# Padding rows copied from HBM, later slots, a first group of four blocks and eight row buffers in a fused attention and mixture-of-experts kernel

## The chip, the core and the metric

The kernel runs on one core of a Trainium2 chip. The metric is the device time of one execution in microseconds; the time before is the median of three runs. One further execution was taken by the hardware profiler. All rows and timelines come from that one, and times in them count from the start of its span.

The core's engines work side by side: PE multiplies matrices (PEld is its weight load), DVE works on vectors, ACT evaluates functions and copies, POOL here mostly starts indirect DMAs, and SP issues the plain DMAs in order on one queue. The DMAs of SP and of POOL are carried by the same 16 DMA engines.

## The reference, cut to what matters

An input of 4 images with 256 channels and 64 x 64 pixels passes two layers. The first normalises and attends over 3 x 3 neighbourhoods. The second treats each of the 16,384 pixels as a token: a gated average over a window of 64 tokens, then a mixture of experts in which each token goes to its best two of eight experts.

```python
logits = tokens @ router_w.T
probs = softmax(logits); rw, re = top_k(probs, 2); rw = rw / rw.sum(-1)
combine = zeros((N, E)).at[arange(N), re].set(rw)
out = tokens
for e in range(E):
    h = gelu(tokens @ w1[e] + b1[e])
    y = h @ w2[e] + b2[e]
    out = out + combine[:, e:e+1] * y
```

All of it is float32.

## The kernel before, in words

**Blocks.** The pixels are cut into 32 blocks (NB) of 512 tokens. A main loop over steps g = 0 to 33 interleaves four generators at their `yield`s: `attend(g)` (first layer), `tail(g - 1)` (window average, store of the block into `out`, choice of experts), `ranks(g - 2)` and `produce(g + 1)`.

**Dispatch.** `ranks` computes for each of a block's 1,024 token-expert pairs a row in an HBM buffer `rows_in`. The buffer has two colours (U = 2) with eight expert regions each, so that the two pairs of one token stand in places that don't collide later. POOL scatters the token rows there with eight indirect DMAs per block (L869, 128 rows each). A row, 1,088 B, holds the 256 values, eight weights and eight copies of the token's number.

**Slots.** The expert work is cut into 136 slots of 256 rows. The generator `experts()` takes slot after slot through these operations, each for a different slot in one pass m:

- `fetch(m + 4)`: SP reads the slot's place from a table and loads its rows into one of seven row buffers `sx` (L1010). It waits until that buffer's former slot has been added.
- `matrix` and `pixels` (m + 2): ACT copies the expert's weights; PE transposes the rows (L1034).
- `hidden(m + 1)`: PE and ACT, first weight and GELU (L1046, L1052).
- `add(m - 1)`: POOL adds two halves of 128 rows to `out` with indirect DMAs (L1082). Each waits until the same half of the slot before has landed.
- `output(m)`: PE second weight (L1065), DVE bias and token weight (L1069, L1070).

A pass has four `yield`s; the passes m = -2 and -1 have two.

**Groups and tables.** A slot's place is known only when enough blocks have been counted. GROUPS gives the number of blocks after which `ranks` writes a new table (L913 to L961): 3, eleven times 2, seven times 1. A group's blocks yield four slots each; the first group has eight fewer, the last 16 more, 20 in all (slots 116 to 135).

**Padding.** Behind the last token row of each of the 16 regions, rows may be fetched that no token fills. In the last block's `ranks`, SP reads 16 places (`values_load`, L898, from `pad`, written at L895) and writes 136 rows of zeros, with token numbers past the end of `out`, to each (L902). Eight copies come from the SBUF tile `blank`, eight from `zeros`, which DVE fills at L794. The fetches of the last group wait for these 16 and for the dispatches.

**Pace.** `follow(at)` runs `experts()` from the main loop. The list `knots` gives, for a position in steps, how many slots are due; between knots it is interpolated. With `done` counting yields:

```python
begins = [at + 2 + LAG for at in first_of[1:]] + [NB + 2.0]
knots = [(at, max(0, n - FETCH - 1)) for at, n in zip(begins, first_slot)]
...
while done < 2 * U * due:
    done += 1
    next(stream, None)
```

FETCH is 2 and LAG 0.35. A step has 26 positions, step 32 has 14 and step 33 eight. What is left of `experts()` is run after the loop. The order on each engine follows this order of the program.

Of the kernel before, what the change touches and what calls it, by code (L numbers as in the profile page):

```python
# [47 lines left out]
FP = mybir.dt.float32  # L48
# [5 lines left out]
P = 128  # L54
# [9 lines left out]
def hybrid_block_kernel(ctx: ExitStack, tc: tile.TileContext, ins: dict, out: bass.AP):  # L64
    nc = tc.nc
    x = ins["x"]
    B, C, HW = x.shape
    W = 64
    NC = C // P
    TB = 512  # L70
    NT = TB // P
    NBI = HW // TB
    NB = B * NBI
    E = ins["w1b"].shape[0]
# [8 lines left out]
    FETCH = 2  # L83
    I32, U32 = mybir.dt.int32, mybir.dt.uint32
    ENG = mybir.EngineType
    GROUPS = (3, *[2] * 11, *[1] * 7)
    assert sum(GROUPS) == NB
    first_of = [sum(GROUPS[:k]) for k in range(len(GROUPS))]
    where = [(k, j) for k, n in enumerate(GROUPS) for j in range(n)]

    U = 2
    UP = U * P
    slots_of = [2 * n * TB // UP for n in GROUPS]
    slots_of[0] -= E
    slots_of[-1] += 2 * E
    assert slots_of[0] > 0
    first_slot = [sum(slots_of[:k]) for k in range(len(GROUPS) + 1)]
    SLOTS = max(slots_of)
    N = B * HW

    PAD = P + E
# [3 lines left out]
    RW = C + 2 * E  # L105
# [7 lines left out]
    w1p = ctx.enter_context(tc.tile_pool(name="w1p", bufs=1))  # L113
    w2p = ctx.enter_context(tc.tile_pool(name="w2p", bufs=2))
    w3p = ctx.enter_context(tc.tile_pool(name="w3p", bufs=3))
    w4p = ctx.enter_context(tc.tile_pool(name="w4p", bufs=4))
    rowp = ctx.enter_context(tc.tile_pool(name="rowp", bufs=7))
    w1sp = ctx.enter_context(tc.tile_pool(name="w1sp", bufs=3))
    hbm = ctx.enter_context(tc.tile_pool(name="hbm", bufs=1, space=bass.MemoryType.DRAM))
    ps_a = ctx.enter_context(tc.tile_pool(name="ps_a", bufs=5, space=PSUM))  # L120
# [140 lines left out]
    for n in range(4):  # L261
        t = const.tile([P, NK + 3], FP, tag=f"logits_{n}", name=f"logits_{n}")
# [36 lines left out]
    def iota(name, shape, pattern, base=0, by_partition=0):  # L299
        t = const.tile(shape, FP, tag=name, name=name)  # L300
        nc.gpsimd.iota(
            t, pattern=pattern, base=base, channel_multiplier=by_partition,
            allow_small_or_imprecise_dtypes=True,
        )
        return t
# [9 lines left out]
    place = iota("place", [P, NT], [[P, NT]], by_partition=1)  # L315
# [15 lines left out]
    blank = const.tile([P, U, RW], FP, tag="blank", name="blank")  # L331
# [3 lines left out]
        float(N),  # L335
    )
    rows_in = hbm.tile([U * HALF, RW], FP, tag="rows_in", name="rows_in")

    def rows_at(at):

        return rows_in.rearrange("(t n) r -> n t r", t=U)[bass.ds(at, P)]
# [100 lines left out]
    def produce(g):  # L442
# [25 lines left out]
        for j in range(0 if i == 0 else 1, NT + 1):  # L468
# [13 lines left out]
        ct[g] = qdotb  # L482
        H = P // 2
        nc.scalar.activation(
            qdotb[0:H, 0:1], first[H:P, C : C + 1], AF.Identity, bias=qbk[H:P]
        )
        nc.scalar.activation(
            qdotb[0:H, 1:NT], v[H:P, 0 : NT - 1, C], AF.Identity, bias=qbk[H:P]
        )
        nc.scalar.activation(qdotb[H:P, :], v[0:H, :, C], AF.Identity, bias=qbk[0:H])  # L490

# [29 lines left out]
    sums, table, norm1 = {}, {}, {}  # L521
# [4 lines left out]
    nc.vector.memset(earlier, 0.0)  # L526
    dispatched = {k: [] for k in range(len(GROUPS))}
    latest = []
# [83 lines left out]
    def tail(g):  # L612
# [143 lines left out]
        both = w2p.tile([P, NT, PAIRS], FP, tag="both", name=f"both_{g}")  # L756
        H, D = E // 2, E // 2 - 1
        at = chosen[:, :, 0, :]
# [4 lines left out]
        )  # L763
        nc.vector.tensor_mul(both[:, :, D * E :], at[:, :, 0:H], at[:, :, H:])

# [18 lines left out]
    def ranks(g):  # L784
        if not 0 <= g < NB:
            return
        k, j = where[g]
        n_blocks = GROUPS[k]
        hot = hots.pop(g)
        chosen, tok = chosens.pop(g), tokens.pop(g)  # L790
        if g == NB - 1:

            zeros = w2p.tile([P, NC, TB], FP, tag="q", name="zeros")
            nc.vector.memset(zeros[:, :, 0:RW], 0.0)  # L794
            nc.vector.tensor_scalar_add(
                zeros[:, :, C + E : RW].bitcast(U32),
                place[:, 0:U].unsqueeze(2).to_broadcast([P, U, E]), float(N + UP),
            )

        yield  # L800

# [16 lines left out]
        nc.vector.tensor_single_scalar(colour[:, :, 1], odd.bitcast(I32), 1, op=ALU.bitwise_and)  # L818
        nc.vector.tensor_scalar(colour[:, :, 0], colour[:, :, 1], -1.0, 1.0, ALU.mult, ALU.add)

        each = w2p.tile([P, 2, NT, U, E], FP, tag="each", name=f"each_{g}")
        for c in range(2):
            nc.vector.tensor_mul(
                each[:, c], hot[:, c].unsqueeze(2).to_broadcast([P, NT, U, E]),
                colour.unsqueeze(3).to_broadcast([P, NT, U, E]),
            )
        by_colour = w2p.tile([P, NT, U * E], FP, tag="by_colour", name=f"by_colour_{g}")
        nc.vector.tensor_add(
            by_colour, *(each[:, c].rearrange("p t k e -> p t (k e)") for c in range(2))
        )  # L830
# [26 lines left out]
        def dispatch(inst):  # L857

            for i in range(k + 1):
                tc.declare_no_dep(  # L860
                    inst, group=f"dispatch_{i}", reason="no two tokens have one row"
                )
            tc.declare_no_dep(inst, group="fetch", reason="fetched rows are not written again")
            tc.add_to_no_dep_group(f"dispatch_{k}", inst)
            dispatched[k].append(inst)
            return inst
# [24 lines left out]
        if final:  # L891


            pad = w2p.tile([1, U * E], I32, tag="pad", name=f"pad_{k}")
            nc.vector.tensor_copy(pad, so_far[0:1, NT, :])  # L895
            H = PAD // U
            for e in range(U * E):
                at = nc.values_load(  # L898
                    pad[0:1, e : e + 1], engines=[ENG.SP], min_val=0, max_val=U * HALF - PAD,
                    skip_runtime_bounds_check_because=IN_RANGE,  # L900
                )
                dispatch(nc.sync.dma_start(  # L902
                    rows_in[bass.ds(at, PAD), :].rearrange("(t p) r -> p t r", p=H),
                    (blank, zeros[:, :, 0:RW])[e // E][0:H],
                ).ins)
            yield

# [41 lines left out]
        )  # L949
        which = small("which", (1, SLOTS))[:, 0:n_slots]  # L950
        nc.vector.tensor_reduce(which, past, AX.X, ALU.add)
        tab = table[k] = w3p.tile([1, 2, SLOTS], I32, tag="tab", name=f"tab_{k}")
        nc.vector.tensor_scalar_min(tab[:, 0, 0:n_slots], which, float(E - 1))
        yield
        nc.vector.tensor_mul(past, past, step.unsqueeze(1).to_broadcast(by_e))
# [170 lines left out]
        pass  # L1126


    STEPS, LAG = {NB: 14, NB + 1: 8}, 0.35
    begins = [at + 2 + LAG for at in first_of[1:]] + [NB + 2.0]  # L1130
    knots = [(at, max(0, n - FETCH - 1)) for at, n in zip(begins, first_slot)]
    stream, done = experts(), 0

# [13 lines left out]
    for g in range(NB + 2):  # L1147
        load_xs(g + AHEAD + 2)
        channel_stats(g + AHEAD)
        gens = [attend(g), ranks(g - 2), tail(g - 1), produce(g + 1)]  # L1150
        if g == 1:
            load_experts()
        n = 0
        while gens:
            for gen in list(gens):
                if next(gen, gens) is gens:
                    gens.remove(gen)
                    continue
                n += 1
                follow(g + min(n / STEPS.get(g, 26), 0.999))  # L1160
# [51 lines left out]
```

## Time and profile before

| What | us |
|---|---|
| median of three runs (1409.02 to 1416.77) | 1412.17 |
| the profiled execution | 1381.8 |
| its span, first to last instruction | 1379.3 |
| PE busy in it | 1248.3 |
| DVE busy | 1051.8 |
| ACT busy | 878.4 |
| POOL busy | 750.7 |
| start of the first slot's fetch (L1010) | 172.3 |
| start of the last add into `out` (L1082) | 1370.5 |

How to read it: a busy time is a sum over the whole span, which has stages with different limits. PE's last matmul ends at about 1355, while the adds go on past 1370. In timeline rows the columns are start, duration, engine, line, operation, out<-in, count, and in brackets the idle time before it and what ended it. Where a wait for several things is put down to an engine, it is the one that came last by the profile; if that engine had long been done, it was another, often a DMA. Rows with SPq are what SP's queue did. Rows of chains give start, duration and what. Rows of stretches give the stretch, its length, the busy time and count of each engine, PE's granted clock as a share of full speed, the busy share of the 16 DMA engines and the bytes they moved.

### The profile page before, as it was taken

How to read it: one execution, taken by the hardware profiler on the slowest of the kernel's cores; microseconds unless marked ns; L12 is line 12 of the kernel's file. 1: busy time of each engine (PE TensorE's matmuls, PEld its weight loads, DVE VectorE, ACT ScalarE, POOL GpSimd, SP SyncE). 2: the span in 40 equal slices, each digit the busy share in tenths (PEclk: the TensorE clock that was granted, in tenths of full speed). 3: DMA queues.
4: the chain of work that ended last, by engine and by line, in shares of the span. 5: the costliest groups of instructions: out<-in, count | busy, mean ns of one | idle time of the engine just before them, and what ended most of it. 6: DMA issues, size and time to landing. Idle time of an engine off the chain costs nothing. (4 is left out here: it accounts for less than half of the span.)

```text
span 1379.3 us, 24259 instructions
## 1 busy us (share of the span) xinstructions
PE 1248.3 (91%) x6380; PEld 999.0 (72%) x6380; DVE 1051.8 (76%) x5159; ACT 878.4 (64%) x1699; POOL 750.7 (54%) x619
## 2 busy tenths in 40 slices
PE   5988797999999999999999999999999999844982
PEld 4766576787787877878888777777877777634762
DVE  4488989898888887888979897888778889721331
ACT  1454466777777778777777776777866776522430
POOL 2004324465655665665666665656666566753665
PEclk8999999999999999999999999999999999976996
DMA  9723345456665666566665645565664555655664
GB/s 320 259 72 118 126 145 158 117 137 149 154 158 131 163 149 149 142 168 138 149 163 115 143 115 139 118 149 135 149 145 83 121 106 131 127 135 108 111 107 49
DMA packets 148679, 191.43 MB, mean 139 GB/s; under 512 B 13760, under 2 KB 122816, under 8 KB 148416
## 3 DMA queue, kind: packets, MB, share of 16 engines
q0 software_dynamic: 51456, 71.34, 29.1%
q1 hardware_dynamic: 94592, 117.10, 27.9%
q10 hardware_dynamic: 2496, 1.45, 0.4%
q8 instruction: 53, 0.87, 0.3%
q14 instruction: 82, 0.67, 0.2%
HBM read 98.59 MB, written 91.25 MB: 138 GB/s over the span
## 5 line engine op out<-in xcount | busy, mean ns | idle before, releaser
L1082 POOL DMA_INDIRECT out<-sx x272 | 451.4, 1660 | 388.6 <-DVE sx L1070 103.8
L869 POOL DMA_INDIRECT rows_in<-tok,rows x256 | 254.4, 994 | 160.0 <-issue 81.7
L1065 PE MATMUL psy<-w,h 128*128 x1088 | 287.9, 387 | 5.8 <-DVE sx L1069 5.4
L1046 PE MATMUL psh<-xc,w1s 128*128 128x256 f32 x1088 | 267.6, 384 | 0.0
L1065 PEld LDWEIGHTS psy<-w,h 128*128 128x128 f32 x1088 | 200.2, 191 | 58.6 <-DVE sx L1069 16.0
L1046 PEld LDWEIGHTS psh<-xc,w1s 128*128 128x128 f32 x1088 | 199.9, 192 | 23.2 <-issue 0.5
L1069 DVE TENSOR_TENSOR sx<-psy,b2b 128x256 f32<-128x256 f32 x272 | 113.9, 419 | 127.5 <-PE psy L1065 121.4
L1052 ACT ACTIVATE h<-psh,w1s 128x256 f32<-128x256 f32 x272 | 114.5, 470 | 100.3 <-PE psh L1046 97.0
L471 PE MATMUL psv<-vo,x 128*128 128x257 f32 x528 | 132.4, 394 | 15.0 <-DVE x L453 13.1
L1034 PE MATMUL ptx<-ident,sx 128*128 128x128 f32 x544 | 84.5, 277 | 56.1 <-DMA sx<-rows_in 55.8
L1038 ACT COPY xc<-ptx 128x512 f32<-128x512 f32 x136 | 80.0, 588 | 81.3 <-PE ptx L1034 81.1
L497 PE MATMUL psq<-x,qk 128*128 128x512 f32 x256 | 126.5, 603 | 0.0
L556 PE MATMUL pss<-x,q 128*128 128x256 f32 x512 | 124.9, 387 | 0.7 <-ACT xc L624 0.7
L1034 PEld LDWEIGHTS ptx<-ident,sx 128*128 128x128 f32 x544 | 66.1, 143 | 79.4 <-DMA sx<-rows_in 35.7
L471 PEld LDWEIGHTS psv<-vo,x 128*128 128x128 f32 x528 | 100.5, 197 | 31.2 <-DVE x L453 10.5
L593 PE MATMUL psc<-v,pT 128*128 128x256 f32 x512 | 121.5, 379 | 0.0
L593 PEld LDWEIGHTS psc<-v,pT 128*128 128x128 f32 x512 | 96.7, 189 | 27.5 <-issue 13.9
L624 ACT COPY xc<-ptx 128x512 f32<-128x512 f32 x64 | 34.3, 589 | 123.8 <-PE ptx L621 123.8
L556 PEld LDWEIGHTS pss<-x,q 128*128 128x128 f32 x512 | 92.4, 190 | 24.3 <-issue 9.7
L1070 DVE TENSOR_SCALAR sx<-sx 128x256 f32<-128x256 f32 x272 | 97.7, 359 | 2.3
L1052 ACT ACT_TABLE_LOAD x77 | 98.8, 1283 | 1.0
L597 DVE SCALAR_TENSOR_TENSOR xT<-psc,den,xT 128x256 f32<-128x256 f32 x128 | 55.8, 475 | 54.2 <-PE psc L593 53.9
(212 smaller groups left out, 2424.3 us busy)
## 6 DMA issues: line engine op xcount, KB each, us to landing
sx<-rows_in SPq DMA_DIRECT2D x136, 272.0 KB
xs<-in_x SPq DMA_DIRECT2D x32, 512.0 KB
xT<-in_xT SPq DMA_DIRECT2D x32, 512.0 KB
out<-xT SPq DMA_DIRECT2D x32, 512.0 KB
x<-in_x SPq DMA_DIRECT2D x24, 640.0 KB
x<-in_x SPq DMA_DIRECT2D x8, 576.0 KB
out<-sx POOLq DMA_INDIRECT x272, 4.2
rows_in<-tok,rows POOLq DMA_INDIRECT x256, 2.6
```

The lines of the kernel that those rows point to most:

```text
L471: nc.tensor.matmul(ps, t[:, ci, j * P : (j + 1) * P], vo[:, ci, :], start=(ci == 0), stop=(ci == NC - 1),)
L497: nc.tensor.matmul(ps, qk[:, ci, co * P : (co + 1) * P], t[:, ci, W : W + TB], start=(ci == 0), stop=(ci == NC - 1),)
L556: nc.tensor.matmul(ps, q[:, ci, t * P : (t + 1) * P], t_[:, ci, t * P : t * P + NK], start=(ci == 0), stop=(ci == NC - 1),)
L593: nc.tensor.matmul(ps[:, u, :], pT[:, u, j, :], vals[j], start=(j == 0), stop=(j == 1))
L869: return nc.gpsimd.indirect_dma_start(out=rows_in[:, :], out_offset=bass.IndirectOffsetOnAxis(ap=rows[:, c, t : t + 1], axis=0), in_=tok[: ...
L1034: nc.tensor.transpose(pt[:, c, t * P : (t + 1) * P], xs[:, t, c * P : (c + 1) * P], ident)
L1046: nc.tensor.matmul(ps[:, f, :], w1s[:, o : o + P], xc[:, ci, :], start=(ci == 0), stop=(ci == NC - 1),)
L1052: inst = nc.scalar.activation(h[:, f, :], ps[:, f, :], AF.Gelu, bias=w1s[:, F1 + f : F1 + f + 1])
L1065: nc.tensor.matmul(ps[:, t, :], h[:, f, t * P : (t + 1) * P], w2[:, e, f, :], start=(f == 0), stop=(f == NC - 1),)
L1069: nc.vector.tensor_add(ys[:, t, :], ps[:, t, :], b2b[:, e, :])
L1070: nc.vector.tensor_scalar_mul(ys[:, t, :], ys[:, t, :], xs[:, t, bass.ds(e + C, 1)])
L1082: inst = nc.gpsimd.indirect_dma_start(out=out, out_offset=bass.IndirectOffsetOnAxis(ap=xs[:, t, C + E : C + E + 1].bitcast(U32), axis=0), ...
```

## The change

Four things are changed. (1) The padding rows stand ready in HBM: at the start two fillers of 136 rows are built in SBUF (POOL and DVE) and written to a new HBM tensor; the 16 pads of the last block copy from there, both sides seen as 17 rows of 8,704 B. The tile `zeros` is gone. (2) The knots lie later and later: a group's slots begin 2.35 steps behind its last block for the first group and 3.0 for the last but one. (3) The first group has four blocks and eight slots, and six single blocks follow in place of seven, so 18 groups in place of 19; there are still 136 slots, the last 20 in the last group. (4) There are eight row buffers in place of seven. To fit, `each` and `by_colour` have one buffer in place of two; `tab` has four in place of three.

```diff
-    GROUPS = (3, *[2] * 11, *[1] * 7)
+    GROUPS = (4, *[2] * 11, *[1] * 6)
...
-    rowp = ctx.enter_context(tc.tile_pool(name="rowp", bufs=7))
+    rowp = ctx.enter_context(tc.tile_pool(name="rowp", bufs=FETCH + 6))
...
+    filler = hbm.tile([U, PAD, RW], FP, tag="filler", name="filler")
+    for k in range(U):
+        t = w2p.tile([P, NC, TB], FP, tag="q", name=f"filler_{k}")[0 : PAD // U, :, 0:RW]
+        nc.gpsimd.memset(t, 0.0)
+        nc.vector.tensor_scalar_add(
+            t[:, :, C + E :].bitcast(U32),
+            place[0 : PAD // U, 0:U].unsqueeze(2).to_broadcast([PAD // U, U, E]),
+            float(N + k * UP),
+        )
+        nc.sync.dma_start(filler[k].rearrange("(t p) r -> p t r", t=U), t)
...
-        if g == NB - 1:
-
-            zeros = w2p.tile([P, NC, TB], FP, tag="q", name="zeros")
-            nc.vector.memset(zeros[:, :, 0:RW], 0.0)
-            nc.vector.tensor_scalar_add(
-                zeros[:, :, C + E : RW].bitcast(U32),
-                place[:, 0:U].unsqueeze(2).to_broadcast([P, U, E]), float(N + UP),
-            )
...
-        each = w2p.tile([P, 2, NT, U, E], FP, tag="each", name=f"each_{g}")
+        each = w1p.tile([P, 2, NT, U, E], FP, tag="each", name=f"each_{g}")
...
-        by_colour = w2p.tile([P, NT, U * E], FP, tag="by_colour", name=f"by_colour_{g}")
+        by_colour = w1p.tile([P, NT, U * E], FP, tag="by_colour", name=f"by_colour_{g}")
...
-            H = PAD // U
             for e in range(U * E):
...
                 dispatch(nc.sync.dma_start(
-                    rows_in[bass.ds(at, PAD), :].rearrange("(t p) r -> p t r", p=H),
-                    (blank, zeros[:, :, 0:RW])[e // E][0:H],
+                    *(r.rearrange("(a b) r -> a (b r)", b=E)
+                      for r in (rows_in[bass.ds(at, PAD), :], filler[e // E]))
                 ).ins)
...
-        tab = table[k] = w3p.tile([1, 2, SLOTS], I32, tag="tab", name=f"tab_{k}")
+        tab = table[k] = w4p.tile([1, 2, SLOTS], I32, tag="tab", name=f"tab_{k}")
...
-    STEPS, LAG = {NB: 14, NB + 1: 8}, 0.35
-    begins = [at + 2 + LAG for at in first_of[1:]] + [NB + 2.0]
+    STEPS, LAST = {NB: 14, NB + 1: 8}, len(GROUPS) - 2
+    begins = [at + 2.35 + 0.65 * k / LAST for k, at in enumerate(first_of[1:])] + [NB + 2.0]
```

## The prediction

> **What bounds the kernel now.** I read the busy time of the engines by stretches first, to find the stage in which time is lost.
>
> ```profile
> core 0: us, PE busy (x) PEld busy (x) DVE busy (x) ACT busy (x) POOL busy (x), PEclk, DMA share, GB/s
> ...
> 500.00:700.00 200.00, 198.10 (x1033) 158.07 (x1033) 172.27 (x849) 150.94 (x282) 122.51 (x93) 1.00 0.62 147
> ```
>
> From about 250 to 1150 us PE is busy 99% of the time at full clock: nothing outside PE can be worth anything there. The same view of the last stage shows where PE stands still.
>
> ```profile
> 1215.00:1225.00 10.00, 8.11 (x38) 6.18 (x36) 3.88 (x10) 3.66 (x8) 7.87 (x8) 1.00 0.68 165
> 1225.00:1235.00 10.00, 0.00 (x0) 0.00 (x0) 0.00 (x0) 0.00 (x0) 4.50 (x4) 0.65 0.53 127
> ...
> 1259.00:1290.00 31.00, 30.99 (x152) 27.23 (x153) 11.26 (x28) 14.19 (x29) 15.53 (x11) 0.95 0.57 105
> 1290.00:1340.00 50.00, 41.68 (x205) 34.14 (x203) 17.05 (x41) 21.64 (x43) 30.98 (x20) 1.00 0.68 110
> ```
>
> The chain that ended last tells why:
>
> ```profile
> 1206.80 7.28 DMA out<-sx x2
> 1214.28 0.37 SPq L1010
> ...
> 1237.60 6.44 DMA rows_in<-zeros
> 1244.04 0.29 issue
> 1244.33 10.86 DMA out<-sx x3
> 1255.46 3.50 DMA sx<-rows_in
> 1259.01 1.12 PE ptx L1034 x4
> ```
>
> From 1214.7 to 1245 SP reads 16 places (L898) and issues 16 pads (L902, 144.5 KB each). The final group's first fetch waits until all have landed (1255.46), PE until 1259.01: 35.3 us of idle.
>
> But PE is not what ends last. Each slot has two adds into `out`, and each add waits for the landing of the same half of the slot before. Counting the 272 adds back from the end (slots 0 to 135; the final group is 116 to 135), POOL's timeline gives for slots 110 to 115, first halves only:
>
> ```profile
> 1226.94 1.60 POOL L1082 DMA_INDIRECT out<-sx  x1 [0.30 <-issue]
> ...
> 1236.60 1.55 POOL L1082 DMA_INDIRECT out<-sx  x1 [6.18 <-DMA out<-sx]
> ...
> 1244.33 1.55 POOL L1082 DMA_INDIRECT out<-sx  x1 [4.13 <-DMA rows_in<-zeros]
> ...
> 1251.66 1.56 POOL L1082 DMA_INDIRECT out<-sx  x1 [3.23 <-DMA out<-sx]
> ...
> 1264.92 1.55 POOL L1082 DMA_INDIRECT out<-sx  x1 [9.19 <-DVE sx L1070]
> ...
> 1269.44 1.55 POOL L1082 DMA_INDIRECT out<-sx  x1 [1.12 <-DVE sx L1070]
> ```
>
> Slot 135 begins at 1368.19, so from slot 114 on a slot takes (1368.19 - 1264.92) / 21 = 4.92 us. PE needs 3.9 (transposes at 1263.63, 1267.52, 1271.41). So adds, not PE, set the pace of the tail: 4.4 to 4.5 us a slot at the very end without fetches, up to 5.5 beside them; I use 5.0. The 38.0 us from slot 110 to 114 hold 18 more than four slots at 5.0. **That 18, not the 35 of PE, is what removing the stall can give.**
>
> **The pads.** The change lets each pad copy 17 runs of 8,704 B from HBM to HBM in place of 68 partitions of two 1,088 B rows. In the stretch 1229 to 1255 us the DMA view says:
>
> ```profile
> q0 software_dynamic: 1033, 1.02, 30.4%
> q1 hardware_dynamic: 1567, 1.66, 19.6%
> ```
>
> q1 (SP's) uses 19.6% of 16 engines for 26 us: 81.5 engine-us for 1.66 MB, 20.4 GB/s per engine. The Trainium skill, "DMA: Bandwidth & Descriptors", section "Why a DMA increments its semaphore by 16 and not by 1", says that a copy is split over the largest number of engines up to 16 that divides the outermost dimension of both sides. For 68 that is 4. A quarter of the adds' 30.4% is 7.6; with 19.6 it makes 27%, about the 25% that four full engines are. So row and rule agree on the old pads. By the same rule 17 is prime, and the new pad goes to ONE engine: 16 x 148 KB / 20.4 GB/s = 116 us. This rule speaks against the change.
>
> What speaks against its use here: both sides of a pad are one unbroken run, and the page says that software can split such a run into a multiple of 16 so that it sprays. Does the builder join dimensions? The page of the profile shows one case:
>
> ```profile
> DMA packets 148679, 191.43 MB, mean 139 GB/s; under 512 B 13760, under 2 KB 122816, under 8 KB 148416
> ...
> q8 instruction: 53, 0.87, 0.3%
> q14 instruction: 82, 0.67, 0.2%
> ```
>
> 263 packets are 8 KB or more. 135 are instruction fetches, which leaves 128: b2b's 128 partitions, written in the code as 8 experts x 1 KB. The two dimensions were joined into 8 KB runs. So I expect the pad's 17 x 8 rows to be joined too and cut for 16 engines: 116 / 16 = 7 us of data. Then issuing binds: the first pads, before the queue filled, came 1.0 us apart (reads at 1214.70, 1215.65, 1216.69), so 16 us in all. I take 16; the other end is 116. No row of before shows a copy from HBM to HBM; the nearest is the pads' own. 2.37 MB read and written in 16 us is 296 GB/s; the first stage's slices show 320, so HBM carries it.
>
> **Later slots.** The due slots are interpolated between the knots. When the last block's ranks reach their second matmul (third yield of eight in step 33, 33.375) the old program owes 109.15 slots, the new one 106.6; at the loop's end 113 and 109. Fetches run four ahead of the steps, so slots up to 115 are fetched ahead of the pads before, up to 111 after. PE per slot is (287.9 + 267.6 + 84.5) / 136 = 4.7 us, so the last block comes 2.55 x 4.7 = 12 us earlier: the place word (L895, 1206.78) at 1194.8, `rows` (1207.7) at 1195.7. The eight row buffers take away the 1214.28 wait (SP held by an add).
>
> What is now behind the pads on SP: the fetches of slots 112 to 115, and PE's transposes for them. SP begins at 1195.2, is done at 1211, slot 112 lands at about 1215 (0.4 issue, 3.3 landing). PE, which took 19 us from that matmul (1204.76) to its stop for 4.85 slots, now has 3.4 slots: it stops at 1192.7 + 13.3 = 1206. So a stall of about 9 us stays in place of 35.3; the four slots before the final group cover the rest.
>
> On POOL: the eight dispatches of the last block (1.3 us each, 1216.67 to 1226.6 before) run from 1195.7 to 1206 behind the add of slot 105, and slot 106 follows at 1206. Slot 110's add is then due at 1226; its data are ready about 7 us after slot 112 lands, at 1222. Margin 4 us: the stall isn't seen. The last add: 1206 + 29 x 5.0 = 1351, plus contention with the pads. Before, three slots lost 4.7 + 2.7 + 2.3 us beside pads that filled four engines; spread over 16 and gone in 16 us I take 3 (bounds 0 and 10). 1354 against 1368.2: **-14 us**. A pace of 4.5 would give 14 more, of 5.3 take 9 back. An eighth buffer lets fetches, hence PE, run one slot further ahead; the adds' pace isn't changed by it.
>
> **What costs nothing, and its cover.** Fillers at the start: two memsets (blank's took 0.54 us), two DVE adds (0.16 to 0.33) and two SP issues of 0.4 between 18.71 and the xT loads at 19.14; 68 partitions, so four engines, 74 KB each: 3.6 us at 20.4 GB/s ahead of the first xT, whose first reader starts at 31.82. Without that cover, 0 to 4 us. First slots a step later: 0.5 slots a step for two steps, then 4, become 2.45, then 4; at 8.4 steps 5.2 slots against 5.0, so PE's total is unchanged: 0, bounds +-5. One group less saves 4 us of small DVE work (78 us over 19 groups), beside PE. `zeros` (0.84 us of DVE at 1118), single buffers for `each` and `by_colour` (next written a block later) and a fourth `tab`: 0.
>
> Sum: 1381.8 (the profiled run; span 1379.3) - 14 = 1368. The median is 1412.17, 1.022 times the profiled run; scaled, -14.3, **1398 us**.
>
> **Rivals.**
> *Pads on one engine (0.16, slower).* Place: SP's queue at step 33; price 116 us. Slot 112's fetch is behind them, from 1195 to about 1315; its adds restart at slot 110 at about 1327 and 25 more take 125: 1452, +84, 1498 us. At the page's ~27 GiB/s per engine 82 us, +50, 1463. It decides once pads take over 20 us, where the 4 us margin is gone. For it: rule and 68-row evidence. Against: b2b's joined rows.
> *The adds take it all (0.22, no change).* Pace 5.3 with one more buffer of fetches beside the adds, or dispatches that delay the chain: -5 to 0, about 1408. For it: adds 7 to 10 us apart beside transfers. Against: 4.92 in the undisturbed tail.
> *More than 14 (0.12).* If the adds run at 4.5: -28, 1383. Against: only the last five slots do so.
>
> The forecast itself has 0.50, own range 1388 to 1405. Over 0.5% (7 us) is about what a measurement can tell from no change. Faster: 0.12 + 0.48 = 0.60; same 0.24; slower 0.16. The range 1380 to 1420 leaves out the one-engine case and little else.
>
> **What would show it.** Right: pads 1.0 us apart, PE's gap near 9 us at slot 112 and none at 116, adds at 5.0 from slot 106 to 135, last add near 1354. Wrong: pads over 5 us apart with SP's share of the 16 engines near 6% (one engine), or adds whose pace isn't 5.0.

## The result and the profile after

| Kernel | median us | ratio to before, 95% interval |
|---|---|---|
| before, 20 runs beside it | 1412.83 | 1 |
| the changed kernel, 20 runs | 1408.11 | 0.9958 [0.9938, 0.9978] |

The forecast was 1398 us; the change brings 0.4%, not 1.0%. The profiled execution of the changed kernel took 1405.04 us (span 1403.3). The profile of before shown above, 1381.8, lies below all of the 20 runs of before that stand here; a second profile of the same program (`b_again` below, span 1402.8) is used wherever after is compared with before.

The pads do what was forecast. The page of the changed kernel:

```profile
DMA packets 147232, 191.73 MB, mean 137 GB/s; under 512 B 13961, under 2 KB 121113, under 8 KB 146713
...
q8 instruction: 53, 0.87, 0.3%
q14 instruction: 83, 0.67, 0.2%
```

Packets of 8 KB or more: 147232 - 146713 = 519. Without 136 instruction fetches and b2b's 128, 255 are left, one short of 16 pads of 16 packets each; the trace itself holds 256 packets of 9,248 B on SP's queue, and 16 of these are one pad. A pad's 17 x 8 rows were joined and cut into 16 equal pieces. In the stretch 1246 to 1272 us the DMA view has (queue, packets, MB, share of 16 engines):

```profile
q0 software_dynamic: 1248, 1.90, 38.0%
q1 hardware_dynamic: 775, 2.65, 36.3%
```

One engine of 16 would have been 6% at most. SP's queue and the stretches of the end:

```profile
1245.91 0.37 SPq L1013 DMA_DIRECT2D sx<-rows_in  x1
1246.80 23.53 SPq L905 DMA_DIRECT2D rows_in<-filler  x16
1271.29 2.98 SPq L1013 DMA_DIRECT2D sx<-rows_in  x3
```

```profile
500.00:700.00 200.00, 198.54 (x1043) 159.00 (x1041) 170.06 (x850) 145.63 (x276) 121.45 (x93) 1.00 0.62 148
...
1255.00:1290.00 35.00, 22.04 (x98) 18.34 (x98) 7.92 (x20) 10.67 (x22) 22.70 (x17) 0.85 0.74 153
1290.00:1340.00 50.00, 45.42 (x230) 38.32 (x229) 19.52 (x46) 23.33 (x47) 32.21 (x21) 1.00 0.71 112
```

The chain of waits, in place of a stop of 35 us:

```profile
1255.09 10.27 issue
1265.37 2.08 PE psy L1068 x4
...
1271.29 3.83 DMA sx<-rows_in
```

And POOL's timeline for slots 107 to 110, first halves (counted back from the end as before):

```profile
1246.10 1.55 POOL L1085 DMA_INDIRECT out<-sx  x1 [3.55 <-DMA out<-sx]
...
1260.02 1.61 POOL L1085 DMA_INDIRECT out<-sx  x1 [0.30 <-issue]
...
1264.62 1.56 POOL L1085 DMA_INDIRECT out<-sx  x1 [1.11 <-issue]
...
1269.97 1.55 POOL L1085 DMA_INDIRECT out<-sx  x1 [1.59 <-issue]
```

From slot 108 on, behind the last dispatch, the adds run to slot 135 (1392.1) without a hole: (1392.1 - 1260.0) / 27 = 4.89 us a slot. So the end of the kernel is as predicted. What is not as predicted is where the end begins: the last block's store (`out<-xT`) is issued at 1240.08, against 1233.95 in the second profile of before. It was forecast 12 us earlier and comes 6 us later.

### The profile page after: what moved, and what is told of

Its sections match the earlier page's. It is cut to its first block, busy times and chain, and to the rows that moved or that the text cites. A ratio compares the mean times of both kernels' runs of the same rounds, so it can differ in the third digit from the quotient of the medians.

```text
span 1403.3 us, 24162 instructions
## 1 busy us (share of the span) xinstructions
PE 1268.3 (90%) x6380; PEld 1001.6 (71%) x6380; DVE 1049.5 (75%) x5138; ACT 864.8 (62%) x1685; POOL 743.6 (53%) x621
## 2 busy tenths in 40 slices
DMA packets 147232, 191.73 MB, mean 137 GB/s; under 512 B 13961, under 2 KB 121113, under 8 KB 146713
## 4 chain that ended last, share of the span: by engine, by line
PE 49%; DVE 14%; DMA 7%; issue 4%; ACT 3%; POOL 0%; another core or an unknown queue 0%; DVEq 0%; POOLq 0%; SPq 0%; ACTq 0%
PE psy L1068 12%; PE psh L1049 10%; PE psc L605 5%; DMA out<-sx 4%; PE psv L483 4%; PE psq L509 4%; PE psw L695 3%; PE pss L568 3%; PE ptx L1037 3%; PE psp L647 2%; DMA sx<-rows_in 2%; DVE tok L710 1%; PE ptp L596 1%; DVE logits L573 1%; DVE sx L1072 1%
## 5 line engine op out<-in xcount | busy, mean ns | idle before, releaser
L1085 POOL DMA_INDIRECT out<-sx x272 | 439.8, 1617 | 394.7 <-DVE sx L1073 82.8
L873 POOL DMA_INDIRECT rows_in<-tok,rows x256 | 257.5, 1006 | 180.8 <-ACT pT L598 94.0
L1068 PE MATMUL psy<-w,h 128*128 x1088 | 291.4, 390 | 27.1 <-issue 15.6
L483 PE MATMUL psv<-vo,x 128*128 128x257 f32 x528 | 140.5, 406 | 14.8 <-DVE x L465 11.2
L1041 ACT COPY xc<-ptx 128x512 f32<-128x512 f32 x136 | 79.7, 586 | 96.1 <-PE ptx L1037 74.9
L568 PE MATMUL pss<-x,q 128*128 128x256 f32 x512 | 127.9, 390 | 10.8 <-issue 7.0
L509 PE MATMUL psq<-x,qk 128*128 128x512 f32 x256 | 122.6, 594 | 0.0
L605 PEld LDWEIGHTS psc<-v,pT 128*128 128x128 f32 x512 | 96.1, 190 | 21.5 <-issue 7.4
L1030 ACT COPY w1s<-w1b 128x514 f32 x136 | 84.2, 622 | 2.7 <-issue 0.2
```

The source lines that it names most:

```text
L483: nc.tensor.matmul(ps, t[:, ci, j * P : (j + 1) * P], vo[:, ci, :], start=(ci == 0), stop=(ci == NC - 1),)
L509: nc.tensor.matmul(ps, qk[:, ci, co * P : (co + 1) * P], t[:, ci, W : W + TB], start=(ci == 0), stop=(ci == NC - 1),)
L568: nc.tensor.matmul(ps, q[:, ci, t * P : (t + 1) * P], t_[:, ci, t * P : t * P + NK], start=(ci == 0), stop=(ci == NC - 1),)
L605: nc.tensor.matmul(ps[:, u, :], pT[:, u, j, :], vals[j], start=(j == 0), stop=(j == 1))
L873: return nc.gpsimd.indirect_dma_start(out=rows_in[:, :], out_offset=bass.IndirectOffsetOnAxis(ap=rows[:, c, t : t + 1], axis=0), in_=tok[: ...
L1068: nc.tensor.matmul(ps[:, t, :], h[:, f, t * P : (t + 1) * P], w2[:, e, f, :], start=(f == 0), stop=(f == NC - 1),)
```

## The experiments

There are three sets of runs, each beside runs of before on its own chip. The first takes the parts of the change one by one, to tell two questions apart: is the profile of before short for its program (A), or does the change lose its gain at the head (B); and which part loses it. The second and third put two theories of the later slots against each other:

- **Phase (C).** A step yields four slots, so a slot's share is 0.25 of a step. The four parts of each slot fall at certain places among the parts of the block. A lag that moves by a fraction of a share moves them to worse places, over the whole middle.
- **Lateness (D).** Beginning later costs by itself, since work is moved behind the last block.

**Before again**, unchanged.

> The kernel before, unchanged, for a second profile. Theory A (the profile of before was a lucky execution: its 1381.8 us lie below all of its timed runs): the new profile's span is near 1410, and the extra 25 to 30 us show as PE idle in the first 400 us, as in the profile of the changed kernel. Theory B (the first slots' delay really costs 20 to 25 us in the head, and the timed runs of before are longer for some other reason): the new profile reaches the ninth store of a block near 383 us again, and what it has more of is in the last stage. Ratio 1.000 by both.

Measured: 1408.74 us, 1.0007 [0.9980, 1.0034]; span 1402.8. On this chip, then, 1379.3 is not a span of this program (A; more on it with the last set). The long middle, PE's columns first (PE busy, PEld busy, each with its count):

```profile
300.00:1000.00 700.00, 689.33 (x3606) 553.45 (x3605) 595.12 (x2959) 527.26 (x984) 429.02 (x324) 1.00 0.60 142
```

**The pads alone.** Before, with the fillers and the copies from HBM; `zeros` is gone.

```diff
-                    rows_in[bass.ds(at, PAD), :].rearrange("(t p) r -> p t r", p=H),
-                    (blank, zeros[:, :, 0:RW])[e // E][0:H],
+                    *(r.rearrange("(a b) r -> a (b r)", b=E)
+                      for r in (rows_in[bass.ds(at, PAD), :], filler[e // E]))
```

> The kernel before with the pads from HBM alone. Pads spread over 16 engines and issued 1.0 to 1.5 us apart end 10 to 20 us earlier; with the adds setting the pace of the tail the gain is 10 to 15 us (0.990 to 0.993); if PE set it, 20 (0.986). The rival that the pads alone gain nothing, since the fetches wait for the last dispatches and the adds anyway: 0.998 to 1.002.

Measured: 1390.32 us, 0.9859 [0.9834, 0.9883]: alone more than three times what the whole change brings. First halves of slots 110 to 114 in `b_again`:

```profile
1251.51 1.60 POOL L1082 DMA_INDIRECT out<-sx  x1 [0.30 <-issue]
...
1260.90 1.55 POOL L1082 DMA_INDIRECT out<-sx  x1 [5.92 <-DMA out<-sx]
...
1269.27 1.55 POOL L1082 DMA_INDIRECT out<-sx  x1 [4.41 <-DMA rows_in<-zeros]
...
1276.88 1.56 POOL L1082 DMA_INDIRECT out<-sx  x1 [3.98 <-DMA out<-sx]
...
1290.28 1.55 POOL L1082 DMA_INDIRECT out<-sx  x1 [9.70 <-DVE sx L1070]
```

and of the same slots with the new pads:

```profile
1252.00 1.60 POOL L1083 DMA_INDIRECT out<-sx  x1 [0.30 <-issue]
...
1256.93 1.55 POOL L1083 DMA_INDIRECT out<-sx  x1 [1.46 <-issue]
...
1262.25 1.55 POOL L1083 DMA_INDIRECT out<-sx  x1 [1.92 <-issue]
...
1266.78 1.56 POOL L1083 DMA_INDIRECT out<-sx  x1 [0.91 <-issue]
...
1273.55 1.55 POOL L1083 DMA_INDIRECT out<-sx  x1 [2.77 <-DVE sx L1071]
```

38.8 us against 21.5: 17.3 us, close to the 18 of the prediction, out of the 19.0 us by which the last add comes earlier (1372.51 against 1391.55). The wait for data of a stopped PE (9.70) shrinks to 2.77, and those beside slow pads (4 to 6) to 1 or 2. But the 1.4%, 20 us, missed the 10 to 15 that I had put for this run; it is the number that I had put for the case that PE sets the pace. PE's first transpose of the final group also comes 16 us earlier (1267.8 against 1283.9), so this run alone doesn't tell the two apart. The middle is as before:

```profile
300.00:1000.00 700.00, 690.30 (x3617) 554.59 (x3616) 594.29 (x2959) 528.29 (x989) 429.17 (x323) 1.00 0.59 142
```

**The later knots alone**, with the fourth `tab`.

```diff
-    begins = [at + 2 + LAG for at in first_of[1:]] + [NB + 2.0]
+    begins = [at + 2.35 + 0.65 * k / LAST for k, at in enumerate(first_of[1:])] + [NB + 2.0]
```

> The kernel before with the later knots alone (and the fourth table buffer). Four slots stand in front of the final group while the slow pads run: PE's gap at the final group shrinks from 35 to under 20 us, but the fetches of those four now stand behind 30 us of pads on SP. My theory, the adds set the pace: 0.993 to 1.000. Rival, the queue behind the slow pads costs more than it covers: 1.002 to 1.010.

Measured: 1428.41 us, 1.0119 [1.0094, 1.0144]. This part makes the kernel slower, by more than the rival had put, and my own theory missed it altogether. Its middle, then that of the changed kernel:

```profile
300.00:1000.00 700.00, 682.31 (x3507) 539.22 (x3506) 583.87 (x2887) 510.72 (x955) 410.34 (x314) 1.00 0.59 138
```

```profile
300.00:1000.00 700.00, 683.47 (x3520) 540.54 (x3519) 582.00 (x2897) 503.75 (x951) 404.24 (x313) 1.00 0.59 138
```

PE is busy for 97.5 and 97.6% of the time, against 98.5% in `b_again`, and yet does 99 and 86 matmuls fewer. At 700 / 3606 = 0.194 us each, with their share of all else, that is 19 and 17 us of work not done. Only about 6 or 7 us of them show as idle time of PE; the rest is matmuls that count as busy for longer (682.31 / 3507 = 0.1946 us each, against 0.1912). The last block's store comes at 1243.52, 9.6 later than in `b_again`, though three slots fewer were added before it (105.5 against 108.5).

**The group alone**: `GROUPS = (4, *[2] * 11, *[1] * 6)` in before.

> The kernel before with the first group of four blocks alone. Theory B: slots start one step later, PE has nothing to fill the early steps with, and the head is 20 us longer: 1.010 to 1.016. Theory A: the head's order doesn't matter, ratio 0.998 to 1.003.

Measured: 1405.51 us, 0.9984 [0.9964, 1.0005]: nothing that can be told from none. So the head loses nothing (B falls). Sum of the parts: -1.41 - 0.16 + 1.19 = -0.38%, against -0.42 measured for the whole. Nothing is left for the eighth row buffer.

The next four kernels are the one with the new pads and four `tab`s, with one edit each.

**Half a share later**: `LAG` 0.475 in place of 0.35, at all groups.

> Pads from HBM, and every group's slots an equal 0.125 of a step later (half a slot's share of a step), so that the four parts of a slot fall between other parts of a block. Theory C (what the later knots cost is the place of the slots' parts among the block's, in the long middle): the weight loads' busy share from 300 to 1000 us falls from the 79.2% of the pads-alone kernel, to under 78%, and the time is 1 to 2% over the 0.986 of the pads alone: 0.993 to 1.005. Theory D (what costs is lateness: fewer slots at hand early on and more left for the end): 0.125 of a step is half a slot, 0.986 to 0.989.

**One share later**: `LAG` 0.60.

> Pads from HBM, every group's slots 0.25 of a step later: one slot's share, so that the same parts meet at nearly the same places. Theory C: the middle is as dense as with the pads alone (79%), 0.986 to 0.991. Theory D: a slot is left for the end, worth 4 to 5 us, 0.989 to 0.993, and the middle is as dense as well. If it is as slow as the half-slot shift, it is neither, and any shift from 0.35 costs.

**A whole step later**: `LAG` 1.35.

> Pads from HBM, every group's slots a whole step later, at the same place within it. Theory C: the middle is as dense as with the pads alone (79% weight loads from 300 to 1000 us); four more slots are left for the end, whose adds go 4.7 us apart where PE's slot in the middle also costs 4.7: 0.985 to 0.993. Theory D: four slots late from the start on, as late as the changed kernel's last groups but everywhere: 0.997 or more, the blocks' stores as late as with the later knots.

**The last single group late**: `begins[-2] = NB + 2.0`, meant to bring its four slots behind the loop without touching the middle.

> Pads from HBM, old knots, but the last but one group's four slots are left for after the loop, so that they stand in front of the final group while its pads and dispatches run. This is the cover of the changed kernel without its later knots in the middle. Pads alone left PE 13 us of wait at the final group's first slot. By theory C and by D the middle is untouched; the cover is worth up to those 13 us, less what the four fetches lose behind the pads on SP: 0.978 to 0.986. If the adds set the pace in this stage as I predicted, nothing: 0.985 to 0.989.

| kernel | lag against before, in shares | us | ratio, interval | matmuls 300 to 1000 us | last block's store |
|---|---|---|---|---|---|
| new pads alone | 0 | 1390.32 | 0.9859 [0.9834, 0.9883] | 3617 | 1233.52 |
| LAG 0.475 | 1/2 | 1430.87 | 1.0089 [1.0054, 1.0125] | 3481 | 1267.44 |
| LAG 0.60 | 1 | 1390.00 | 0.9808 [0.9770, 0.9845] | 3625 | 1230.23 |
| LAG 1.35 | 4 | 1403.23 | 0.9890 [0.9850, 0.9930] | 3601 | 1220.42 |
| last single group late | 0, but for one group | 1398.63 | 0.9875 [0.9854, 0.9897] | 3605 | 1235.99 |

Half a share costs 2.3% (1.0089 / 0.9859), a whole share, twice as far, costs nothing, and four shares come out 0.3% above none by the ratios, which the intervals don't separate. Two of the sizes that C had named were missed (1.0089 lies above its 1.005, 0.9808 below its 0.986), but the order is that of C. On the same chip the half share takes 40.9 us more than the whole one. So the phase is what costs; lateness alone doesn't reach the 0.997 that D asked for at LAG 1.35. It isn't free either: on the same chip four shares take 13 us more than one (0.9890 against 0.9808). The two lines to see are those of LAG 0.475 and of LAG 0.60:

```profile
300.00:1000.00 700.00, 682.11 (x3481) 535.65 (x3480) 577.30 (x2852) 493.52 (x940) 404.84 (x311) 1.00 0.59 138
```

```profile
300.00:1000.00 700.00, 692.12 (x3625) 556.01 (x3624) 597.60 (x2982) 528.97 (x992) 428.26 (x325) 1.00 0.61 143
```

The last single group late did not do what it was meant for. In its trace 116 slots are fetched ahead of the pads and 26 slots are added behind the last dispatch, both as with the new pads alone, and PE still waits 10.05 us for the final group's rows. So its 0.9875 says nothing about a cover. LAG 1.35 has the cover: 112 slots are fetched ahead of the pads, PE waits 9.16 us for the rows of slot 112 and not at slot 116. It gains nothing by it. From slot 106 to 135 its adds go 5.2 us apart, and PE waits again and again for rows on the way. There the adds set the pace and not PE, as predicted.

The last set ran on a third chip, on which before takes 1384.23 us; only its ratios are compared with the others.

**One and a half shares later**: `LAG` 0.725, with the new pads. It asks whether 0.475 is a bad place by chance, or half shares are in general.

> The old knots with LAG 0.725, one and a half slot shares later, beside the new pads. Theory of the phase, with a period of one slot's share (0.25 of a step): as dear as LAG 0.475, ratio 1.00 to 1.015 and about 3480 matmuls between 300 and 1000 us. If only 0.475 was unlucky by itself, and not half a share in general: like LAG 0.60, 0.98 to 0.985 with 3610 or more.

Measured: 1395.51 us, 1.0081 [1.0054, 1.0108], 3531 matmuls in the middle. The ratio came as the phase has it; the matmul count is 50 above what I had named for it, on a chip where the dense kernels have 3638 and 3647.

**The changed kernel, growing in whole shares only**: lags of 0.35, 0.60, 0.85 and 1.10.

```diff
-    begins = [at + 2.35 + 0.65 * k / LAST for k, at in enumerate(first_of[1:])] + [NB + 2.0]
+    begins = [at + 2.35 + 0.25 * round(2.6 * k / LAST) for k, at in enumerate(first_of[1:])] + [NB + 2.0]
```

> The changed kernel with lags that still grow, but only in whole slot shares: 0.35, 0.60, 0.85 and 1.10. Theory of the phase: nearly all slots keep their place in the block, only the intervals at the two or three jumps are stretched, so 3590 matmuls or more between 300 and 1000 us and a ratio of 0.98 to 0.988. Theory of the drift (that growing later is itself what costs, since the steps then hold less than four slots each): like the changed kernel, 0.995, with about 3520 matmuls.

Measured: 1363.63 us, 0.9844 [0.9830, 0.9857], 3609 matmuls. The same growth, in steps that keep the phase, doesn't cost: 0.9844 in place of the change's 0.9958.

**The changed kernel with a constant lag of 0.60.**

> The changed kernel with one constant lag of 0.60 of a step at all knots (one slot's share later than before) in place of lags that grow from 0.35 to 1.0. Theory of the phase: what made the later knots dear is where a slot's parts fall among the block's parts; a whole slot's share keeps that place, so the middle is as dense as before (3600 matmuls or more between 300 and 1000 us, against 3520 in the changed kernel) and the pads' gain stays: ratio 0.979 to 0.985. Theory that being later costs by itself: about 0.99 to 0.995. If the eighth row buffer or the larger first group is worth something, below 0.979.

Measured: 1363.35 us, 0.9854 [0.9840, 0.9867], 3638 matmuls: at the very end of what the phase gives (0.985), and no sign of a gain from the eighth buffer.

**The changed kernel with the old knots** (LAG 0.35, and three `tab`s again).

> The changed kernel with the old knots (LAG 0.35 at all groups): new pads, first group of four blocks and eight row buffers. If the parts add up and the eighth buffer is worth nothing: 0.9859 x 0.9984 = 0.984, so 0.981 to 0.988. If the eighth buffer helps once the pads are short, it is below 0.98.

Measured: 1361.70 us, 0.9838 [0.9822, 0.9854], by the product of the parts 0.9859 x 0.9984 = 0.9843. By the ratios this version beats both kernels: 1.6% below before, 1.2% below the changed one (0.9838 / 0.9958). Between it, the two above, the new pads alone and LAG 0.60, the intervals don't choose.

**What stands late in the wrong phase.** Between 300 and 1000 us, by line (count, busy, mean ns, idle before and what ended it), of the changed kernel with the old knots and then of LAG 0.725, on the same chip:

```profile
L807 PE MATMUL psk<-upto_t,before 128*128 128x28 f32 x38 | 7.1, 268 | 0.7
L1053 ACT ACTIVATE h<-psh,w1s 128x256 f32<-128x256 f32 x152 | 63.9, 470 | 22.4 <-PE psh L1047 21.7
```

```profile
L807 PE MATMUL psk<-upto_t,before 128*128 128x28 f32 x38 | 7.5, 277 | 8.2 <-DVE upto_t L780 8.1
L1053 ACT ACTIVATE h<-psh,w1s 128x256 f32<-128x256 f32 x146 | 62.5, 472 | 117.0 <-PE psh L1047 116.3
```

PE reaches a matmul of `ranks` (L807) while DVE is still at its operand `upto_t`, and all that is queued behind it on PE waits. At LAG 0.475 the same row has 8.2, too, in place of 0.7. ACT's pause, which in the good phase lies elsewhere, stands in front of the GELU. These 8 us are one of the places where time goes, of some 22 ((3647 - 3531) x 0.192) to 26 ((3617 - 3481) x 0.194).

A second place is in `tail`, which has eight pairs of matmuls per block (`psw`, L694 and L695). The two halves of a pair start some 7 ns apart and run side by side for 0.4 us. At LAG 0.725 the second weight of a slot (L1066) stands between the halves of two pairs:

```profile
703.32 0.61 PE L694 MATMUL psw<-wl,bandl 128*64 128x265 f32 x2
703.86 1.13 PE L1066 MATMUL psy<-w,h 128*128 x4
704.92 0.66 PE L695 MATMUL psw<-wx,band 128*64 128x265 f32 x2
```

In the text of the program the two lines of a pair follow each other, so the order on PE isn't wholly the program's. How often this happens, and how often PE waits over 1 us for `upto_t`, marks the phase (counts of 300 to 1000 us, 144 to 152 pairs):

| lag | pairs split | waits over 1 us |
|---|---|---|
| 0.35, 0.60 or 1.35 (nine profiles) | 0 | 0 |
| growing in whole shares | 4 | 1 |
| the changed kernel | 20 | 1 |
| the later knots alone | 20 | 4 |
| 0.475 | 26 | 8 |
| 0.725 | 26 | 8 |

Counted from start to start of PE's matmuls, LAG 0.725 loses 22.5 us against the changed kernel with the old knots: 8.9 in front of `upto_t`'s matmul, 5.6 at the pairs, and the rest in small sums over many lines. In the changed kernel (against `b_again`) the two places hold 5 of 17 us; 5.4 more stand in front of the transposes of `xT` (L633). That a half share is dear, and a whole one not, is shown; which of these waits causes which is not.

The drift shows as waves. With the later knots alone, split pairs stand from 309 to 541 us and from 804 to 1042, none between. The lag there is about 0.40 to 0.51 and 0.64 to 0.76, which takes in 0.475 and 0.725, and between them it passes 0.60 (worked out from the stores of the blocks and the formula of the knots). The matmuls follow, against `b_again` on the same chip: 958 against 1024 from 250 to 450 us, and then

```profile
450.00:750.00 300.00, 296.80 (x1550) 237.96 (x1549) 252.84 (x1255) 225.50 (x424) 179.45 (x139) 1.00 0.62 147
750.00:1050.00 300.00, 289.84 (x1471) 226.90 (x1470) 248.73 (x1242) 209.77 (x394) 175.04 (x133) 0.99 0.55 126
```

against 1545 and 1528. In the changed kernel the split pairs stand from 267 to 506 us and from 800 to 1067. Its matmuls follow less cleanly: it is 83 short from 250 to 550 us (1453 against 1536), and from 750 to 1050 it has 1531, no fewer than `b_again`, though 15 fewer from 850 to 950. Part of its early shortfall stands in the kernel with the group alone, too (982 from 250 to 450, in place of 1024), which makes it up later.

## Why the prediction was half right

**Pads on all 16 engines: right.** Rows above. The rule that would have put each on one engine, in the Trainium skill, "DMA: Bandwidth & Descriptors", section "Why a DMA increments its semaphore by 16 and not by 1", goes by the pattern "as the instruction carries it". The packets above show that the 17 of the source text wasn't that pattern any more. b2b's rows on the page of before were the right evidence.

**Pads 1.0 us apart, 16 us: mis-sized here.** They took 23.53 us in the changed kernel and 22.25 with the pads alone, 1.4 to 1.5 us apart. On the third chip they took 18.11 and 16.51, about what I had forecast from a profile of 1379.3 us. The shown profile of before thus looks like one from a chip of that kind, on which before takes 1384. The head says the same: the seventh block's store is issued at 272.04 us in it, at 269.90 in the changed kernel with the old knots on the third chip, and at 289.01 in `b_again`. Its chip isn't recorded, so that stays a guess.

**18 us in the adds: right.** 17.3 between slots 110 and 114, with the pads alone. **A slot at 5.0 us in the tail: right**, 4.89.

**A stop of about 9 us of PE, hidden from the adds: right in size by luck** (10.27). It was to come from the fetches of slots 112 to 115, held up behind the pads on SP. But 115 slots, not 112, are fetched ahead of the pads in the changed kernel (116 before), so slot 115 alone was held up, for 2.17 us of PE; the 10.27 stand in front of a slot's output. The count of slots from the knots, "up to 111 after", was wrong.

**Nothing from the first group, the eighth buffer: right** as far as the intervals tell. The fillers were never run without the new pads.

**The step that failed** is that of the later slots: "PE per slot is (287.9 + 267.6 + 84.5) / 136 = 4.7 us, so the last block comes 2.55 x 4.7 = 12 us earlier". It treats PE as a bag of work from which slots can be taken out at their price. The sentence from which it starts holds the same error: "From about 250 to 1150 us PE is busy 99% of the time at full clock: nothing outside PE can be worth anything there". Putting the slots off by whole shares does make the last block come earlier (1230.23 and 1220.42 against 1235.99 on the same chip), but the drifting lag spoiled the interleaving of slots and blocks, and the last block came 6 us later, where 12 us earlier was forecast.

In sums: two slots fewer before the last block should give 2 x 4.7 = 9 us; instead the store came 6 us later, so some 16 us were lost in the middle, as the 86 matmuls say. Even without that loss, 28 slots follow the last dispatch in place of 26, which at 4.9 takes the 9 us back. By my own pace the later knots had nothing to give: what was to be won was won by the pads alone. In my sum of -14 the stall's -18 and the knots' part, about nothing, stood unseparated, and so I did not see that the knots could only lose.

What should have warned me is a rule of the skill which I did not weigh: "Perfetto Trace Analysis", section "Identifying the Most-Contended Engine", holds matmul busy time a poor measure of how near PE is to its limit, and would go by the FLOPs and the weight loads. Here the weight loads agree: 553.45 of 700 us in `b_again` (79.1%) and 540.54 (77.2%) after fall by 1.8 points, where PE's own busy time moved from 98.5 to 97.6%, by 0.8.

**The rivals.** Pads on one engine: no. "The adds take it all" (0.22) has the right time, about 1408, and the wrong cause: its pace of 5.3 didn't come, and the adds gave their 18. *More than 14* (0.12) names what the pads give alone, 20 us, but its reason, a pace of 4.5, didn't come (4.7 from slot 114 on).

## What to carry to other kernels

A busy share of 99% on PE does not mean that an edit elsewhere is free: here an edit that left PE 97.6% busy did 86 matmuls fewer in 700 us. Count matmuls per stretch, or take the share of the weight loads, before and after. Where two streams are interleaved on engines that work in order, a shift of one against the other is a change of phase: try it in whole periods and in half ones before asking what "later" is worth. And a change of four parts is worth its parts' runs: here one gave 1.4% and another took 1.2% of it back.

## What was not expected of the hardware

- One program, three chips: before took 1408.37, 1415.24 and 1384.23 us. The pads' reads and issues by SP took 22 to 24 us on the first kind and 16.5 to 18 on the last. Why the chips differ was not tried.
- A copy of 144.5 KB from HBM to HBM, 16 of them in a row: 36.3% of the 16 engines over 26 us for SP's 2.65 MB, of which 2.37 are the pads, or 2.65 MB / (0.363 x 16 x 26 us) = 17.5 GB/s for each engine, beside 38.0% of the adds and dispatches. The old pads from SBUF had 20.4.
